# Attention's TensorE work written out in rounds of like forms, with score products that alternate between row halves

## The chip, the cores and the metric

The kernel runs on one core of a Trainium2 chip. The time is that of one execution on the device in microseconds; the median of three runs stands for the kernel. The core's engines work side by side, each through its own queue: TensorE (PE in the profile, with its weight loads as PEld), VectorE (DVE), ScalarE (ACT), GpSimd (POOL) and SyncE (SP), which here only issues DMAs. [...]

## The reference

Four blocks follow each other, each adding to x of 4 x 256 rows with 512 columns: attention, a feed-forward block with a choice of clusters, a state-space mixer over a sequence of 256, and the feed-forward block again. The change touches attention only:

```python
x = x + attn_a(layernorm(x))     # 4 batches, 256 queries, 32 heads of 16
# attn_a: q, k, v = split(x @ w_attn.T); rotary on q and k
#   y  = softmax(causal(q k^T / 4)) @ v
#   y += gating * softmax(q ak^T / sqrt(512)) @ av     # 10 adapter keys
#   return y @ w_proj.T
x = x + ffn(layernorm(x))
x = x + mixer(layernorm(x))
x = x + ffn(layernorm(x))
```

## The kernel before

Everything is float32. To keep accuracy at a higher rate, most operands are split into two fp32r parts (`split`, L104 and L105), and a product of split operands is three products (`mm3`, L112 to L114). The mixer, which takes the larger part of the time, and the last feed-forward block lie behind attention and are the same in both kernels.

Attention handles one batch b after another. A batch has eight steps u of four heads each, so there are 32 of them (`i` in the loop). For each pair of steps `pieces` (L380, L382) turns stacked parts of q and k so that four head pairs stand on partitions: 64 rows are one head with its parts, so two heads (`pr` 0 and 1) lie in the upper and lower half of the partitions.

One step consists of these parts, and each lags behind the one before it by a step:

- `scores`: for each half c of the queries and each row half pr, two products of 64 rows against all 256 keys (L425) into one PSUM tile sc, then the causal mask as one product in bf16 with the identity (L429). VectorE takes the maximum (L434), and ScalarE two exponentials with their sums (L437). For c = 0 only the first 128 keys are read.
- `turn`: twelve transposes of the exponentials (ptr, L452) in three PSUM tiles, two copied by VectorE and one by ScalarE (L453).
- `weigh`: eight value products (py, L462 and L468), each in one quarter of the array's columns, and a copy by ScalarE (ys, L473).
- `gathered`: two transposes back (try, L479), division by the sums (L485).

In every second step there are the adapter's scores (pa, L390, copied as sa, L394, turned as tra, L397). Beside this, generators give further work. `prepared(b + 1)` normalises the next batch and projects it to q, k and v (tr and pq; rotary reads pq three times on VectorE, L281 to L285). `adapter` makes the adapter's keys and values once (pk, pv). `adapted(b)` makes the softmax over the adapter's scores and its products (L496 to L520: pt, paT, pya, ya). `closed` and `ended` turn the finished y and project it (L530, po). `fed` runs the feed-forward block of finished tiles (pd).

The order in which the program is written is not the order in which engines work. A planner of the framework orders each engine's instructions, with its own costs and due times, and so mixes the parts of several steps on every engine. PSUM is divided into pools: `ps` with two buffers (tag "m") for most products, `ps_s` with three for sc, `ps_t` with two for ptr and `ps_y` with one for py. A tile takes its pool's buffers in turn and waits until the last reader of its buffer is done.

Of the kernel before, what the change touches and what calls it, by code (L numbers as in the profile page):

```python
# [20 lines left out]
P = 128  # L21
# [5 lines left out]
NA = 10  # L27
# [50 lines left out]
def hybrid_kernel(  # L78
# [153 lines left out]
    def attention(later):  # L232
        with ExitStack() as es:
# [6 lines left out]
            ps = pool("a_m", 2, space=PSUM)  # L240
            ps_s = pool("a_s", 3, space=PSUM)
            ps_t = pool("a_t", 2, space=PSUM)
# [114 lines left out]
            def prepared(b):  # L357

                where = (ps, "m") if b else (ps_s, "sc")
                xs = []  # L360
                for c in range(2):
                    xs.append(normed(norm, 2 * b + c))
                    yield
                    for f, w in ((0, wq_s), (1, wk_s)):
                        qk[b, c, f] = rotated(projected(xs[c], w, where), c, f, f"r{f}{c}")
                        yield
                for c in range(2):
                    nc.scalar.copy(vs[b % 2][:, c, :C], projected(xs[c], wv_s, where))
                    yield
# [16 lines left out]
            def adapter_scores(b, q):  # L386
# [6 lines left out]
                sa = p1.tile([AW, 4, P], F32, name="sa", tag="paT").rearrange("p s i -> p (s i)")[:, :L]  # L393
                nc.scalar.copy(sa, pa)  # L394
                tr = ps.tile([P, 2, AW], F32, name="tra", tag="m")
# [8 lines left out]
            def begin(b):  # L404
                state[b] = {
                    "as": p2.tile([P, 2, NH, NA], F32, name="as"),
# [6 lines left out]
            def scores(b, u):  # L413
# [4 lines left out]
                for c in range(2):  # L418
                    n = (c + 1) * P
                    for pr in range(2):  # L420
                        rows = slice(64 * pr, 64 * pr + 64)
                        sc = ps_s.tile([P, 2, L], F32, name="sc", tag="sc")
                        for j in range(2):
                            blk = (u % 2) * 2 + j
                            nc.tensor.matmul(  # L425
                                sc[:, j, :], qT[rows, blk, c * P : (c + 1) * P], kT[rows, blk, :],
                                start=(j == 0), stop=False,
                            )
                        nc.tensor.matmul(  # L429
                            sc[:, :, n - P : n], identb, negb.unsqueeze(1).to_broadcast([P, 2, P]),  # L430
                            start=False, stop=True,
                        )
                        nm = p3.tile([P, 2], F32, name="nmx", tag="nmx")
                        nc.vector.tensor_reduce(nm, sc[:, :, :n], AX.X, ALU.max, negate=True)  # L434
                        for j in range(2):
                            h = 4 * u + 2 * j + pr
                            nc.scalar.activation(  # L437
                                es_[c][:, 2 * j + pr, :], sc[:, j, :n], AF.Exp,
                                bias=nm[:, j : j + 1], accum_out=rs[:, c, h : h + 1],
                            )  # L440
                return es_

            def turn(es_):
# [3 lines left out]
                for src, k, dst in (  # L447
                    (es_[0], 0, e0[:, :, :P]), (es_[1], 0, e0[:, :, P:]), (es_[1], 1, e1)
                ):
                    pt = ps_t.tile([P, 4, P], F32, name="ptr", tag="pt")  # L450
# [39 lines left out]
            def adapted(b):  # L490
# [13 lines left out]
                yield  # L504
                for c in range(2):
# [6 lines left out]
                    paT = p1.tile([80, 4, P], F32, name="paT", tag="paT")  # L512
                    nc.scalar.copy(paT, pt)
                    pa = ps.tile([P, C], F32, name="pya", tag="m")
                    for s in range(4):
                        nc.tensor.matmul(
                            pa[:, s * P : (s + 1) * P], paT[:, s, :], avbd[:, s, :],
                            start=True, stop=True,
                        )
                    nc.scalar.copy(st["ya"][:, c, :], pa)  # L520
                    yield

            def closed(b, k):

                st = state[b]
                y = st["y"][:, :, k * P : (k + 1) * P]
                nc.vector.tensor_tensor(y, y, st["ya"][:, :, k * P : (k + 1) * P], ALU.add)
                tr = ps.tile([P, L], F32, name="try2", tag="m")
                for c in range(2):
                    nc.tensor.transpose(tr[:, c * P : (c + 1) * P], y[:, c, :], ident)  # L530
                split([v[:, k, :] for v in st["yT"]], tr)

            def ended(b):
# [27 lines left out]
            def fed(f, t):  # L561
                xs = normed(f.norm, t)
                yield
                f.tile(t, xs, [ps.tile([P, FH], F32, name="pd", tag="m") for _ in range(2)])
                yield
# [32 lines left out]
            def adapter():  # L598
                split(wt, wte_s)
                adapter_weights()  # L600
                adapter_scores(0, 0)
                yield
                adapter_values()
                yield
# [3 lines left out]
            for i in range(n + 3):  # L608
                if i < n:
                    b, u = divmod(i, 8)  # L610
                    if u == 0:
                        begin(b)
                        pieces(b, 0)
                        if i == 0:
                            jobs.append(adapter())
                        if b + 1 < B:
                            jobs.append(prepared(b + 1))
                    if u == 6:
                        jobs.append(adapted(b))
                    es_[i] = scores(b, u)  # L620
                    if u % 2 == 0 and i > 0:
                        adapter_scores(b, u // 2)
# [587 lines left out]
```

## Time and profile before

| | |
|---|---|
| median of three runs | 1920.82 us (1916.88 to 1924.34) |
| the profiled execution | 1916.66 us |
| its span, first to last instruction | 1914.9 us |
| granted TensorE clock over the span | 0.990 |
| first score product, start of the 32nd step, count of clusters | 36.1, 352.2 and 395.1 us |
| busy from 40 to 364 us: PE, DVE, ACT, POOL | 321.2, 203.2, 210.7, 52.3 us |

The profile's page gives each engine's busy time and its share of the span, then the span in 40 slices of 47.9 us as digits in tenths. Groups of instructions are named by line, engine, operation and tiles, result first. Each has its count, its busy time, the mean duration of one, and the idle time before it with the engine that ended it. Durations of products overlap, as TensorE works on several at once; how fast they follow each other is seen from their start times in the timeline. In a timeline's row stand start, duration from the first start to the last end of the merged instructions, engine, line, operation, tiles, shape and count. A product of two fp32 operands that is not a transpose stands there as two records.

### The profile page before, as it was taken

Reading aid. Unit: us, or ns where it says so; the run is one execution under the profiler, and the core shown is the slowest. Engines: PE = TensorE matmul, PEld = TensorE weight load, DVE = VectorE, ACT = ScalarE, POOL = GpSimd, SP = SyncE. Lnnn points to the kernel's source line nnn. Section 1 sums busy time; section 2 is a strip of 40 time slices with the busy share of each in tenths; the row PEclk is TensorE's granted clock in tenths of the full one; section 3 lists DMA queues with packets and bytes.
Section 4 is the critical chain, followed back from the end, with each engine's and each line's share of the span. In section 5 each row is a group of like instructions: output and inputs, shape, how many; then the busy total and the mean of one; then the engine's idle time right before and its main releaser. Section 6 shows DMA issues by size and latency. Waiting matters only on the chain.

```text
span 1914.9 us, 29954 instructions
## 1 busy us (share of the span) xinstructions
PE 1866.0 (97%) x10690; PEld 1468.9 (77%) x10690; DVE 1475.2 (77%) x2324; ACT 1383.2 (72%) x2873; POOL 361.0 (19%) x308
## 2 busy tenths in 40 slices
PE   7999999989999999999999999999999999999997
PEld 6767767767777787888787878877777788787786
DVE  5556657678998777877877797778777877877777
ACT  5665667557898677876787787778677877786753
POOL 4212120011331111222111121212111211131100
PEclk7999999989999999999999999999999999999999
DMA  4000000014455554544455454446454554455341
GB/s 141 1 1 1 1 21 24 12 38 155 169 192 184 160 168 140 160 154 160 149 164 161 149 172 156 148 147 187 149 165 154 160 159 160 138 166 162 119 123 49
DMA packets 151909, 240.35 MB, mean 126 GB/s; under 512 B 12368, under 2 KB 77520, under 8 KB 151760
## 3 DMA queue, kind: packets, MB, share of 16 engines
q1 hardware_dynamic: 151760, 238.44, 39.1%
q8 instruction: 84, 1.38, 0.3%
q14 instruction: 65, 0.53, 0.1%
HBM read 202.75 MB, written 35.65 MB: 124 GB/s over the span
## 4 chain that ended last, share of the span: by engine, by line
PE 84%; DVE 6%; ACT 4%; DMA 2%; issue 1%; SPq 0%; DVEq 0%; ACTq 0%
PE pp L112 12%; PE pp L113 11%; PE pp L114 11%; PE pyy L928 8%; PE pog L112 6%; PE pog L114 6%; PE pog L113 6%; PE sc L425 3%; PE trx L913 3%; PE ptr L452 2%; DVE acc L854 2%; PE py L462 1%; PE sc L429 1%; PE trp L380 1%; DMA wor<-in_wout_dram 1%
## 5 line engine op out<-in xcount | busy, mean ns | idle before, releaser
L112 PE MATMUL pp<-mx,w 128*128 128x512 f32 (+1 forms) x1160 | 465.6, 401 | 8.4 <-DVE acc L854 7.9
L114 PE MATMUL pp<-mx,w 128*128 128x512 f32 (+1 forms) x1160 | 454.2, 392 | 0.0
L113 PE MATMUL pp<-mx,w 128*128 128x512 f32 (+1 forms) x1160 | 454.2, 392 | 0.0
L854 DVE SCALAR_TENSOR_TENSOR acc<-pp,cw_s,acc 128x1012 f32<-128x1012 f32 (+2 forms) x240 | 304.8, 1270 | 23.1 <-ACT acc L847 22.4
L902 DVE TENSOR_TENSOR em<-em,gm 128x1536 f32<-128x1536 f32 x128 | 228.4, 1785 | 94.3 <-ACT em L896 86.0
L112 PEld LDWEIGHTS pp<-mx,w 128*128 128x128 f32 x1160 | 218.6, 188 | 66.0 <-issue 9.9
L114 PEld LDWEIGHTS pp<-mx,w 128*128 128x128 f32 x1160 | 218.5, 188 | 45.5 <-issue 0.4
L113 PEld LDWEIGHTS pp<-mx,w 128*128 128x128 f32 x1160 | 218.9, 189 | 40.7 <-issue 0.7
L890 POOL TENSOR_SCALAR_AFFINE_SELECT r<-r 128x512 f32<-128x512 f32 x128 | 144.6, 1129 | 526.6 <-DMA r<-cumd 418.5
L951 POOL TENSOR_TENSOR sq<-sq,acc 128x1024 f32<-128x1024 f32 x55 | 132.6, 2410 | 581.8 <-ACT acc L950 581.8
L104 ACT CAST w<-wr 128x512 fp32r<-128x512 f32 x144 | 88.5, 615 | 187.6 <-PE pp L113 164.4
L112 PE MATMUL pog<-wo,gh 128*128 128x512 f32 x512 | 204.3, 399 | 0.0
L114 PE MATMUL pog<-wo,gh 128*128 128x512 f32 x512 | 200.3, 392 | 0.0
L113 PE MATMUL pog<-wo,gh 128*128 128x512 f32 x512 | 199.9, 390 | 0.0
L895 ACT ACTIVATE em<-r,col_t 128x128 f32<-128x128 f32 x512 | 165.0, 391 | 48.2 <-PE pyy L928 46.5
L928 PE MATMUL pyy<-em,xd 128*64 128x256 f32 (+1 forms) x2048 | 189.1, 330 | 2.4 <-DVE em L902 2.4
L928 PEld LDWEIGHTS pyy<-em,xd 128*64 128x64 f32 x2048 | 134.2, 137 | 63.6 <-issue 21.7
L898 ACT ACTIVATE em<-r,col_t 128x128 f32<-128x128 f32 x512 | 166.5, 389 | 0.0
L886 DVE TENSOR_SCALAR em<-r,col_t 128x128 f32<-128x128 f32 x512 | 137.1, 327 | 12.1 <-PE pyy L928 10.1
L914 DVE TENSOR_TENSOR xd<-trx,dt_t 128x512 f32<-128x512 f32 x128 | 86.2, 683 | 54.6 <-PE trx L913 54.4
L105 DVE TENSOR_TENSOR w<-wr,w 128x512 fp32r<-128x512 f32 x139 | 97.4, 702 | 37.8 <-ACT w L104 37.3
L437 ACT ACTIVATE e<-sc,nmx 128x128 f32<-128x128 f32 (+1 forms) x256 | 105.2, 424 | 15.0 <-DVE nmx L434 14.9
(287 smaller groups left out, 3313.4 us busy)
## 6 DMA issues: line engine op xcount, KB each, us to landing
wr<-in_win_dram SPq DMA_DIRECT2D x287, 256.0 KB, 2.8
r<-cumd SPq DMA_DIRECT2D x128, 512.0 KB, 4.1
spill<-gb SPq DMA_DIRECT2D x63, 512.0 KB, 2.8
gr<-spill SPq DMA_DIRECT2D x120, 256.0 KB, 3.5
wor<-in_wout_dram SPq DMA_DIRECT2D x64, 256.0 KB, 3.1
out_dram<-x SPq DMA_DIRECT2D x8, 256.0 KB, 2.3
x<-in_x_dram SPq DMA_DIRECT2D x1, 1536.0 KB, 10.2
gr<-spill SPq DMA_DIRECT2D x8, 192.0 KB, 2.5
```

The costliest lines, as they stand in the source:

```text
L112: nc.tensor.matmul(o, lh, rh, start=(first and k == 0), stop=False)
L113: nc.tensor.matmul(o, lh, rl, start=False, stop=False)
L114: nc.tensor.matmul(o, ll, rh, start=False, stop=(last and k == n - 1))
L437: nc.scalar.activation(es_[c][:, 2 * j + pr, :], sc[:, j, :n], AF.Exp, bias=nm[:, j : j + 1], accum_out=rs[:, c, h : h + 1],)
L854: nc.vector.scalar_tensor_tensor(av[:, :, d:], pv[:, :, : L - d], cw_s[:, ch, tap : tap + 1], av[:, :, d:], ALU.mult, ALU.add,)
L886: nc.vector.tensor_scalar(e[:, b, 2, :], rv[:, b, 1, :], col_t[:, h, b, 1:2], 0.0, ALU.subtract, ALU.min,)
L890: nc.gpsimd.affine_select(rv[:, :, 0, :], rv[:, :, 0, :], pattern=[[0, B], [1, P]], compare_op=ALU.is_ge, fill=-1e30, base=0, channel_mult ...
L895: nc.scalar.activation(e[:, b, 1, :], rv[:, b, 1, :], AF.Exp, bias=col_t[:, h, b, 2:3])
L898: nc.scalar.activation(e[:, b, 0, :], rv[:, b, 0, :], AF.Exp, bias=col_t[:, h, b, 0:1])
L902: nc.vector.tensor_tensor(e, e, gm, ALU.mult)
L928: nc.tensor.matmul(py[d, b, k * P :], xd[:, 2 * b + k, d], es2[hh][:, b, 2 * k : 2 if k == 0 else 3, :].rearrange("p s i -> p (s i)"), sta ...
L951: (nc.gpsimd if n < NB - 1 else nc.vector).tensor_tensor(sq, sq, x2, ALU.add)
```

## The change

The diff does four things.

1. Inside `tc.manual_schedule` TensorE's instructions keep the order in which the program writes them. The other engines are still ordered by the planner. The loop is written as rounds: scores; one long job (`step("long", i)`: a projection, the output projection, a feed tile, adapter keys or values); the adapter's scores; the transposes of the round before; back transposes; further transposes (`step("turn", i)`); the adapter's value products; the value products of two rounds before in one run; the next pieces. A generator moves at most one stage in a round.
2. In `scores` the eight products come in a run, c = 1 first, alternating between the two row halves, which write to two PSUM tiles. Then come the four masks. For c = 0 the products take only the first 128 keys, and the tile is half as wide.
3. PSUM: `ps` gets three buffers and takes the ptr tiles too, `ps_s` gets four, `ps_t` goes.
4. Smaller ones: sa and paT have two buffers, the adapter's scores (as) one, nmx six; both copies of paT come ahead of the products pya; `closed` takes the turns of three parts together and includes `ended`; the feed-forward block is set up two rounds later (`n - 6`), and its tiles are begun one in a round from round 28 on. The pieces of the next batch's first pair are made in round 6 of the batch before.

```diff
-            ps = pool("a_m", 2, space=PSUM)
-            ps_s = pool("a_s", 3, space=PSUM)
-            ps_t = pool("a_t", 2, space=PSUM)
+            ps = pool("a_m", 3, space=PSUM)
+            ps_s = pool("a_s", 4, space=PSUM)
...
-                sa = p1.tile([AW, 4, P], F32, name="sa", tag="paT").rearrange("p s i -> p (s i)")[:, :L]
+                sa = p2.tile([AW, 4, P], F32, name="sa", tag="paT").rearrange("p s i -> p (s i)")[:, :L]
                 nc.scalar.copy(sa, pa)
+                yield
                 tr = ps.tile([P, 2, AW], F32, name="tra", tag="m")
...
-                for c in range(2):
+                made = []
+                for c in (1, 0):
                     n = (c + 1) * P
-                    for pr in range(2):
-                        rows = slice(64 * pr, 64 * pr + 64)
-                        sc = ps_s.tile([P, 2, L], F32, name="sc", tag="sc")
-                        for j in range(2):
-                            blk = (u % 2) * 2 + j
+
+                    pair = [ps_s.tile([P, 2, n], F32, name="sc", tag="sc") for _ in range(2)]
+                    for j in range(2):
+                        blk = (u % 2) * 2 + j
+                        for pr in range(2):
+                            rows = slice(64 * pr, 64 * pr + 64)
                             nc.tensor.matmul(
-                                sc[:, j, :], qT[rows, blk, c * P : (c + 1) * P], kT[rows, blk, :],
-                                start=(j == 0), stop=False,
+                                pair[pr][:, j, :], qT[rows, blk, c * P : (c + 1) * P],
+                                kT[rows, blk, :n], start=(j == 0), stop=False,
                             )
-                        nc.tensor.matmul(
-                            sc[:, :, n - P : n], identb, negb.unsqueeze(1).to_broadcast([P, 2, P]),
-                            start=False, stop=True,
+                    made += [(c, pr, sc) for pr, sc in enumerate(pair)]
+                for c, pr, sc in made:
+                    n = (c + 1) * P
+                    nc.tensor.matmul(
+                        sc[:, :, n - P :], identb, negb.unsqueeze(1).to_broadcast([P, 2, P]),
+                        start=False, stop=True,
+                    )
+                    nm = p3.tile([P, 2], F32, name="nmx", tag="nmx", bufs=6)
+                    nc.vector.tensor_reduce(nm, sc, AX.X, ALU.max, negate=True)
+                    for j in range(2):
+                        h = 4 * u + 2 * j + pr
+                        nc.scalar.activation(
+                            es_[c][:, 2 * j + pr, :], sc[:, j, :], AF.Exp,
+                            bias=nm[:, j : j + 1], accum_out=rs[:, c, h : h + 1],
                         )
...
-                    pt = ps_t.tile([P, 4, P], F32, name="ptr", tag="pt")
+                    pt = ps.tile([P, 4, P], F32, name="ptr", tag="m")
...
+            with tc.manual_schedule(engines={nc.tensor.engine}):
+                for i in range(n + 7):
                     b, u = divmod(i, 8)
-                    if u == 0:
-                        begin(b)
-                        pieces(b, 0)
+                    if i < n:
                         if i == 0:
-                            jobs.append(adapter())
-                        if b + 1 < B:
-                            jobs.append(prepared(b + 1))
...
+                        es_[i] = scores(b, u)
+                    if i == n - 6:
+                        inner.close()
...
+                    if slow and i >= n - 4:
+                        begun(slow.pop(0))
+                    step("long", i)
+                    if i < n and u % 2 == 0 and i > 0:
+                        asides.append(adapter_scores(b, u // 2))
+                        next(asides[-1])
+                    if 1 <= i <= n:
+                        eTs[i - 1] = turn(es_.pop(i - 1))
+                    if 3 <= i < n + 3:
+                        gathered(*divmod(i - 3, 8), yss.pop(i - 3))
+                    while asides:
+                        next(asides.pop(0), 0)
+                    step("turn", i)
+                    if i < n and u == 7:
+                        begun(adapted(b))
+                    step("values", i)
+                    if 2 <= i <= n + 1:
+                        yss[i - 2] = weigh(*divmod(i - 2, 8), eTs.pop(i - 2))
...
+                    if i < n and u % 2 == 0:
+                        if u < 6:
+                            pieces(b, u // 2 + 1)
+                        elif b + 1 < B:
+                            pieces(b + 1, 0)
```

## The prediction

> **What bounds the kernel now.** I read the page first: busy shares, then the slices, then the costliest groups.
>
> ```profile
> PE 1866.0 (97%) x10690; PEld 1468.9 (77%) x10690; DVE 1475.2 (77%) x2324; ACT 1383.2 (72%) x2873; POOL 361.0 (19%) x308
> PE   7999999989999999999999999999999999999997
> PEclk7999999989999999999999999999999999999999
> ```
>
> TensorE is busy 97% of the span and in slices 1 to 7 (48 to 383 us), where attention lies, nearly all the time. The change touches attention alone: its first score product starts at 36.1 us (of the 1914.9) and its last step, the count of clusters, at 395.1. So 359 us are at stake; the mixer behind them keeps its work. The next question is who makes TensorE wait there. The list of waits between 48 and 364 us, for TensorE alone, is all of this:
>
> ```profile
> PE pya L516 <- ACT paT L513: 0.7, 1, 0.7
> PE sc L425 <- ACT e L437: 0.3, 1, 0.3
> PE ptr L452 <- ACT e L437: 0.2, 1, 0.2
> PE ptr L452 <- DVE eT L453: 0.2, 1, 0.2
> ```
>
> It waits 1.4 us in 316. Attention is bound by what TensorE is given and by the order it gets it in. Busy is not the same as streaming, though, and this is read from start times in the timeline (start, duration, what):
>
> ```profile
> 80.97 0.62 PE L462 MATMUL py<-eT,av 128*32 128x256 f32 x2
> 81.52 0.36 PE L397 MATMUL tra<-con,sa 80*128 80x80 f32 x2
> 81.81 0.42 PE L462 MATMUL py<-eT,av 128*32 128x256 f32 x3
> ...
> 82.59 0.44 PE L479 MATMUL try<-con,ys 128*128 128x128 f32 x2
> ...
> 91.46 0.64 PE L462 MATMUL py<-eT,av 128*32 128x256 f32 x8
> 91.91 0.40 PE L468 MATMUL py<-eT,av 128*32 128x128 f32 x8
> 92.25 0.44 PE L479 MATMUL try<-con,ys 128*128 128x128 f32 x2
> ...
> 95.41 0.50 PE L425 MATMUL sc<-pc,pc 64*128 64x256 f32 x2
> 95.84 0.28 PE L429 MATMUL sc<-negb,identb 128*128 128x256 bf16 x1
> 96.06 0.50 PE L425 MATMUL sc<-pc,pc 64*128 64x256 f32 x2
> 96.49 0.28 PE L429 MATMUL sc<-negb,identb 128*128 128x256 bf16 x1
> 96.70 0.50 PE L425 MATMUL sc<-pc,pc 64*128 64x256 f32 x2
> ```
>
> One score group (two products of 64 rows, one mask) repeats every 0.64 us (96.06 to 96.70). The products hold 0.43 of it: in the trace the second starts 0.22 behind the first and the mask 0.21 behind the second. A 256-column product in full-array form repeats in 0.12 (the adapter's pa, L390). So about 0.10 per product is not streaming: the weights of a product in the same half are loaded after the product before it, and each change between the 64-row and the full form costs about 0.10. The value products py show the same: in one piece they hold 0.79 us (91.46 to 92.25); cut in two by the planner they hold 0.55 + 0.78 = 1.33 (80.97 to 81.52, 81.81 to 82.59).
>
> **The change, part by part.** A round is one u of one batch; there are 32.
>
> *Scores.* Today four groups, 4 x 0.645 = 2.58 us. After: eight products in a run, alternating between the halves, then four masks in a run. No row of this trace has two row halves side by side. The nearest is py, whose four column quarters start 5 to 7 ns apart in the trace, so they run at once. If halves behave so, each half repeats in 0.22 and two products are done in it. Products with all keys: 2 x 0.22 = 0.44. Those of the first queries now stream 128 columns; load 0.11 + stream 0.06 = 0.17 per pair, 0.34. With 0.10 to enter the form: 0.88. Masks 4 x 0.11 = 0.44. Together 1.32, saving 1.26 a round, 40 us in all. If halves merely hide each other's loads, one product every 0.11, it is the same 0.88. If they share nothing, 8 x 0.22 = 1.76: the saving is 12.
>
> *128 columns.* An fp32r product this narrow is not in the trace. [...]
>
> *Value products.* Always in one piece: 0.79 and 0.09 to enter, against 1.33 or more; 0.5 x 32 = 16 us. TensorE's own saving: 40 + 16 = 56.
>
> *What fixed order and buffers give back.* Now the planner fills TensorE's gaps. After, it stands in its queue. PSUM goes from 2 + 3 + 2 + 1 banks to 3 + 4 + 1: transposed weights (ptr), projections, pieces (trp), adapter and transposes share three buffers in turn. I walk a round from its first score product, in us; a round's eight exponentials follow each other by 0.45 (256 columns) or 0.34 (128), 3.16 in all, beginning 1.85 after it (products, mask, 0.6 of maximum), so they end at 5.0.
>
> - Rounds with a projection: scores to 1.3, twelve products at 0.233 to 4.1. VectorE reads pq three times, 1.3 us, to 5.65. The third of the next uses of the buffers is a ptr group at about 5.0: it waits 0.7. Some 18 rounds: 13 us. The projection is the cover: it carries TensorE past the exponentials, behind which ScalarE's copies sa and eT stand.
> - Even rounds without one (8, 16, 24, 26): pa is done at 1.8, but its copy sa stands on ScalarE behind the exponentials until 5.35. The third ptr group needs that buffer and waits from 2.7 to 5.4; behind it stand try, the adapter's transposes, py and the next pieces. About 3 us each with what follows: 12.
> - Adapter softmax, once per batch: maximum 0.81, POOL 1.29, exponential 0.74 stand in ScalarE's order ahead of the copies of the pieces; about 1 each, 4.
> - Round 0: pk comes right behind the first masks (now at 47.5), but the adapter weights take 6.6 us from its end to the last copy (51.0 to 57.6) with TensorE's queue behind them. Some of it is won back as pk comes 8 us sooner (clock, below): net 3.
>
> Other moves: the buffer swaps (as to one, paT to two, six nmx) cost nothing while nobody reads the old copy that late. Feed tiles start in round 28 instead of 24, so 144 of their 192 products follow the last round's scores, in place of 72: from that round's first score to the count it is 42.9 us today (352.2 to 395.1), and after, by the rows above, 38 of work and today's 6 of idle, so nothing. DMA issues stay the same ones on SP's queue; those of the feed weights come two rounds later, still three rounds ahead of their use (they land in 3.6 us).
>
> Sum: 56 - (13 + 12 + 4 + 3) = 24 us. The profiled execution took 1916.7 (span and 1.8 around it) and goes to 1892.7; the median of the runs is 4.2 above, 1920.8 to 1896.8. I say 1896.
>
> [...] The clock first, from the windows view (us, busy PE, PEld, DVE, ACT, POOL with counts, clock, DMA):
>
> ```profile
> 32.00:36.00 4.00, 1.77 (x12) 1.40 (x12) 2.60 (x3) 1.95 (x6) 2.95 (x5) 0.87 0.00 2
> 36.00:48.00 12.00, 11.50 (x45) 7.97 (x45) 5.39 (x11) 8.03 (x30) 0.92 (x3) 0.50 0.00 1
> 114.00:137.00 23.00, 22.91 (x181) 16.17 (x179) 14.36 (x30) 18.41 (x64) 2.30 (x5) 1.00 0.00 1
> ```
>
> [...] Rounds 24 to 27 will have transposes, scores and py but no projection for about 30 us. From 36 to 48 such a mix did stay at 0.50 after the idle of 32 to 36. From 114 to 137 the same mix without one wide projection kept 1.00. [...]
>
> **Rivals.**
> (A) The waits are hidden: copies come in time, three buffers suffice. Speaking for it: DVE and ACT are busy only 203 and 211 of the 324 us from 40 to 364. Against: the copies' order behind the exponentials. 56 less 5: 1870.
> [...]
> (C) The halves share nothing: 12 + 16 - 32, 1925. For it: within one half a product takes 0.22; against: the quarters of py run at once.
> (D) Slower. One mechanism: TensorE in its fixed order waits for ScalarE's copies behind the exponentials, in every round, not only the light ones. It decides above 56 / 32 = 1.75 us a round; at 2.5 it is 80 us and 1945. For it: today's order has 1.4 us of waits because the planner moves other work in; against: a projection of 2.8 us stands between scores and copies in most rounds.
>
> **How the numbers follow.** My forecast 45% (own range 1880 to 1908), A 20%, B 15%, C 12%, D 8%. Measured no change is within 0.5%, 1911.2 to 1930.4, since the runs of the kernel before spread by 0.4%. Faster: 45 + 20 + 13 of B = 78. Same: 2 of B, 8 of C = 10. Slower: the rest, 12. The range for 8 in 10 runs from 1862, below A, to 1926, C's middle and the narrow products at their high price.
>
> **What would show it.** Right: scores of a round with masks in about 1.3 us, products of the two halves starting within some 10 ns or 0.11 apart; py near 0.8; TensorE's list of waits in attention at 25 to 40 us, led by sa, eT and the projection's reads on VectorE; the count near 371. Wrong: the 128-column products more than 0.2 apart; clock 0.50 after round 8; waits over 60 us, or under 10.

## The result and the profile after

The changed kernel takes 1903.41 us, the kernel before, timed beside it, 1919.88: a ratio of 0.9915, 95% interval 0.9901 to 0.9929. It is 16.5 us faster. The forecast was 1896 and its range 1862 to 1926. The profiled execution spans 1900.1 us, 14.8 less than before.

The page of the changed kernel: busy time, the slices of 47.5 us each, and the shares of the chain of work that ended last.

```profile
PE 1817.5 (96%) x10690; PEld 1452.2 (76%) x10690; DVE 1477.0 (78%) x2324; ACT 1381.4 (73%) x2873; POOL 350.2 (18%) x308
PE   7988889889999999999999999999999999999997
PEclk8999999989999999999999999999999999999999
PE 77%; DVE 9%; ACT 8%; DMA 2%; issue 2%; POOL 1%; SPq 0%; DVEq 0%; ACTq 0%; POOLq 0%
```

The last of these lines for the kernel before:

```profile
PE 84%; DVE 6%; ACT 4%; DMA 2%; issue 1%; SPq 0%; DVEq 0%; ACTq 0%
```

TensorE is busy 48.5 us less than before (1866.0), and the kernel is only about a third of that faster. In the slices of attention, where there were nines, there are now eights: TensorE waits. The chain ran over TensorE for 84% of the span before; now it is 77%, and the copying engines have taken the rest (DVE 6 to 9, ACT 4 to 8).

What TensorE's time in attention consists of is worked out from start times: a product is charged with the time from its start to the start of the next one, less idle over 70 ns, which is charged to waits. "Wide" are products of 512 or 288 columns (projections, feed). The stretch runs from the first score product to the count of clusters; behind it both kernels take 1520 to 1521 us. The last column is the time, from start to start, of the products that started at a granted clock of 0.50. All in us; each ratio is to the kernel before as timed beside that kernel. The experiments stand here too and are told below.

| kernel | median, ratio to before | stretch | score | mask | py | wide | other | waits | at 0.50 |
|---|---|---|---|---|---|---|---|---|---|
| before | 1919.9 | 359.1 | 58.8 | 19.5 | 41.5 | 110.1 | 120.8 | 8.3 | 12.7 |
| after | 1903.4, 0.9915 | 343.5 | 20.8 | 13.3 | 27.3 | 108.7 | 132.2 | 41.3 | 26.5 |
| e1, halves in turn | 1904.0, 0.9914 | 345.0 | 21.6 | 13.2 | 27.1 | 110.4 | 131.1 | 41.6 | 29.2 |
| e6, all keys | 1904.5, 0.9917 | 343.5 | 22.5 | 12.6 | 27.1 | 109.0 | 131.3 | 41.0 | 23.1 |
| e8, new scores in the kernel before | 1907.5, 0.9938 | 350.3 | 48.4 | 17.9 | 37.0 | 113.1 | 124.8 | 9.1 | 24.1 |
| e2, planner's order | 1896.9, 0.9876 | 337.8 | 39.4 | 14.4 | 39.5 | 108.8 | 122.9 | 13.0 | 10.2 |
| e10, planner, runs kept whole | 1901.6, 0.9907 | 337.8 | 20.8 | 13.1 | 25.9 | 106.2 | 130.7 | 41.1 | 15.8 |
| e12, fourth shared buffer | 1884.2, 0.9818 | 326.1 | 20.3 | 13.2 | 26.2 | 111.0 | 123.8 | 31.5 | 26.7 |
| e7, rounds 24 to 27 filled | 1901.6, 0.9909 | 343.6 | 20.4 | 12.6 | 26.1 | 109.2 | 137.7 | 37.6 | 20.0 |
| e4, feed early | 1899.8, 0.9894 | 340.8 | 20.3 | 12.7 | 26.9 | 108.5 | 131.8 | 40.5 | 23.2 |
| e14, e12 and e4 | 1876.1, 0.9777 | 317.0 | 20.4 | 13.5 | 25.4 | 108.3 | 123.2 | 26.3 | 19.9 |
| e13, e12, e4 and e2 | 1873.6, 0.9763 | 313.8 | 36.5 | 15.0 | 25.4 | 105.9 | 118.4 | 12.7 | 8.3 |

So scores, masks and value products gave 58.4 us, waits took 33.0 of it back and the other work 10.0 (other +11.4, wide -1.4). The difference, 15.4, is the gain.

Most of those 10.0 belong to the waits as well. The last product ahead of a wait is charged with its whole duration (a ptr with 273 ns, where without a wait the next one starts 118 ns after it). There are 84 such products after and 17 before, and what they are charged above the mean of their kind is 11.9 us after and 2.5 before. So waits delayed TensorE by 42.4 us more than before, and 33.0 is the idle part of it.

The list of waits of the changed kernel between 36 and 379 us, TensorE alone, its first seven rows: what waited, for whom, us in total, times, longest.

```profile
PE try L484 <- DVE eT L458: 6.0, 9, 1.0
PE ptr L457 <- DVE t L284: 4.0, 6, 0.7
PE ptr L457 <- DVE eT L458: 3.9, 6, 1.0
PE tra L332 <- POOL st L305: 2.5, 2, 1.7
PE try L484 <- ACT av L368: 2.4, 3, 0.8
PE ptr L457 <- ACT av L368: 2.1, 3, 0.7
PE ptr L457 <- ACT sa L393: 2.1, 5, 0.7
```

All but the fourth are a tile in the shared pool with tag "m" of PSUM, where TensorE's products land; the releaser in each of their rows is a step that reads an older tile of that pool (eT reads ptr, t and av read pq, sa reads pa; in round 8, below, VectorE's first copy ends at 113.41 and the waiting ptr group starts at 113.47). None of them is longer than 1.7 us; they are many small ones, in nearly every round.

One round, number 8, is a light one without a projection. The timeline of the changed kernel: TensorE from its first score product to the next round's (start, duration, what, count, idle before and its releaser).

```profile
109.94 0.67 PE L427 MATMUL sc<-pc,pc 64*128 64x256 f32 x8
110.54 0.61 PE L434 MATMUL sc<-negb,identb 128*128 128x256 bf16 x4
110.91 0.73 PE L389 MATMUL pa<-pc,akbd 128*80 128x256 f32 x4
111.47 1.04 PE L457 MATMUL ptr<-con,e 128*128 128x128 f32 x8
113.47 0.66 PE L457 MATMUL ptr<-con,e 128*128 128x128 f32 x4 [0.96 <-DVE eT L458]
114.15 0.41 PE L484 MATMUL try<-con,ys 128*128 128x128 f32 x2
115.21 0.36 PE L397 MATMUL tra<-con,sa 80*128 80x80 f32 x2 [0.65 <-DVE ry L489]
115.40 1.04 PE L515 MATMUL pt<-con,as 128*80 128x128 f32 x8
116.68 0.66 PE L163 MATMUL tr<-con,axn 128*128 128x128 f32 x4 [0.23 <-ACT paT L519]
117.26 0.64 PE L467 MATMUL py<-eT,av 128*32 128x256 f32 x8
117.72 0.40 PE L473 MATMUL py<-eT,av 128*32 128x128 f32 x8
118.05 1.85 PE L379 MATMUL trp<-con,st 128*128 128x128 f32 x16
119.83 0.38 PE L427 MATMUL sc<-pc,pc 64*128 64x256 f32 x2
```

And the same stretch on ScalarE:

```profile
114.44 0.40 ACT L442 ACTIVATE e<-sc,nmx 128x128 f32<-128x128 f32 x1
114.69 0.24 ACT L442 ACTIVATION_READ_ACCUMULATOR e<-sc,nmx 128x1 f32 x1
114.78 0.38 ACT L393 COPY sa<-pa 80x256 f32<-80x256 f32 x1
115.03 0.61 ACT L458 COPY eT<-ptr 128x512 f32<-128x512 f32 x1
```

Eight score products come in one run; first product to first mask is 0.60 us, the masks to pa another 0.37. Two ptr groups begin together, the third waits 0.96 for VectorE's copy of the first, which stands behind the four maxima:

```profile
110.86 1.95 DVE L439 TENSOR_REDUCE nmx<-sc 128x2 f32<-128x512 f32 x4 [1.08 <-PE sc L434]
112.73 1.28 DVE L458 COPY eT<-ptr 128x512 f32<-128x512 f32 x2
```

The adapter's transposes tra wait 0.65. The trace puts that down to ry on VectorE, but sa, which they read, is copied at 114.78, behind the last exponential, and ends at 115.16: that is what released them at 115.21, 0.05 later.

### The profile page after: what moved, and what is told of

The parts are those of the page before. It is cut to its first block, busy times and chain, and to the rows that moved or that the text cites. A ratio compares the mean times of both kernels' runs of the same rounds, so it can differ in the third digit from the quotient of the medians.

```text
span 1900.1 us, 29893 instructions
## 1 busy us (share of the span) xinstructions
PE 1817.5 (96%) x10690; PEld 1452.2 (76%) x10690; DVE 1477.0 (78%) x2324; ACT 1381.4 (73%) x2873; POOL 350.2 (18%) x308
## 4 chain that ended last, share of the span: by engine, by line
PE 77%; DVE 9%; ACT 8%; DMA 2%; issue 2%; POOL 1%; SPq 0%; DVEq 0%; ACTq 0%; POOLq 0%
PE pp L112 12%; PE pp L113 12%; PE pp L114 11%; PE pyy L961 8%; PE pog L112 6%; PE pog L114 6%; PE pog L113 6%; PE trx L946 3%; ACT e L442 3%; DVE acc L887 2%; DMA wor<-in_wout_dram 1%; PE ptr L457 1%; PE sc L427 1%; DVE nmx L439 1%; PE py L467 1%
## 5 line engine op out<-in xcount | busy, mean ns | idle before, releaser
L887 DVE SCALAR_TENSOR_TENSOR acc<-pp,cw_s,acc 128x1012 f32<-128x1012 f32 (+2 forms) x240 | 304.9, 1270 | 23.2 <-ACT acc L880 22.6
L112 PEld LDWEIGHTS pp<-mx,w 128*128 128x128 f32 x1160 | 218.5, 188 | 65.6 <-issue 10.2
L923 POOL TENSOR_SCALAR_AFFINE_SELECT r<-r 128x512 f32<-128x512 f32 x128 | 133.7, 1045 | 542.8 <-DMA r<-cumd 441.2
L442 ACT ACTIVATE e<-sc,nmx 128x256 f32<-128x256 f32 (+1 forms) x256 | 103.7, 431 | 24.9 <-DVE nmx L439 24.9
```

What stands on the lines that cost most here:

```text
L112: nc.tensor.matmul(o, lh, rh, start=(first and k == 0), stop=False)
L442: nc.scalar.activation(es_[c][:, 2 * j + pr, :], sc[:, j, :], AF.Exp, bias=nm[:, j : j + 1], accum_out=rs[:, c, h : h + 1],)
L887: nc.vector.scalar_tensor_tensor(av[:, :, d:], pv[:, :, : L - d], cw_s[:, ch, tap : tap + 1], av[:, :, d:], ALU.mult, ALU.add,)
L923: nc.gpsimd.affine_select(rv[:, :, 0, :], rv[:, :, 0, :], pattern=[[0, B], [1, P]], compare_op=ALU.is_ge, fill=-1e30, base=0, channel_mult ...
```

## Experiments

All are edits of the changed kernel, but for e8, which edits the kernel before.

### Is it the alternation of the halves? (e1)

```diff
-                for c in (1, 0):
-                    ...
-                    for j in range(2):
-                        for pr in range(2):
+                for pr in range(2):
+                    rows = slice(64 * pr, 64 * pr + 64)
+                    for c in (1, 0):
+                        for j in range(2):
```

The four products of the upper half come first, then the four of the lower.

> Same eight score products, masks behind them and fixed order, but all four of the upper row half first, then the four of the lower one. In the changed kernel the pairs of the two halves start 3 to 4 ns apart, 0.22 us behind the pair before (256 columns) and 0.11 (128). Theory (the halves run at once and that is where the score saving lies): each half then takes 0.22 + 0.22 + 0.11 alone and the second follows the first, some 0.65 more in a round, 32 x 0.65 = 21 us, less what lies in waits anyhow: 15 to 21 slower than the changed kernel, 1918 to 1925. Rival (the gain comes from grouping products and masks, fewer changes between the 64-row and the full form): 5 us or less, up to 1908.

Measured: 1904.04 us against 1903.41, ratios 0.9914 and 0.9915. So the alternation is not what pays. The timeline of e1 shows a run of nearly the same length (0.63 from its start to the first mask, where the changed kernel has 0.60):

```profile
164.84 0.70 PE L428 MATMUL sc<-pc,pc 64*128 64x256 f32 x8
165.47 0.61 PE L435 MATMUL sc<-negb,identb 128*128 128x256 bf16 x4
```

The starts inside one such run, in ns from its first product (worked out from the trace):

```
after  (halves alternate)   0   3 | 222 226 | 342 345 | 402 405 | mask 608
e1     (upper, then lower)  0  13 | 222 236 | 341 353 | 401 414 | mask 617
before (one half, two products)  0   224 | mask 432
```

In the kernel before two products of one half start 0.22 apart. In e1 products start in pairs 13 ns apart although the second half's first product stands four places behind the first half's first. The widths say the same: in the program the upper half's two narrow products stand ahead of the lower half's two wide ones, but in all 32 runs of e1 the four wide ones start first and the four narrow ones behind them. So in these runs the starts of one half did not wait for the products of the other that stand ahead in the program. (A trace names neither the half nor the place in the queue; the reading rests on TensorE being given the order of the program, as item 1 of the change has it.) The first step of a half is 0.22 in all three; what the longer run adds is that the later ones are 0.12 and 0.06. What the changed kernel and e1 have in common is that eight products of both halves stand in one run without a mask between them; score takes 20.8 and 21.6 us there, against 58.8 before.

### What are the narrow products worth? (e6)

```diff
-                    pair = [ps_s.tile([P, 2, n], F32, name="sc", tag="sc") for _ in range(2)]
+                    pair = [ps_s.tile([P, 2, L], F32, name="sc", tag="sc") for _ in range(2)]
...
-                                kT[rows, blk, :n], start=(j == 0), stop=False,
+                                kT[rows, blk, :], start=(j == 0), stop=False,
```

The first queries get products with all 256 keys again; only the first 128 columns are read.

> The changed kernel with the first queries' products over all 256 keys again, in tiles of full width; fixed order and runs stay. [...]

Measured: 1904.48, ratio 0.9917 (0.9901 to 0.9933): 1.1 us above the changed kernel, where the author had estimated some 7 for the wider products, less what waits take in. A run takes 674 ns to its first mask against 608, so the narrow products save 0.066 us a round, 2 us in all (score 22.5 against 20.8), and the median does not show it. In the changed kernel a narrow pair is followed after 60 ns, a wide one after 120. Only this one step of a run gets shorter, and the high price of narrow products that the range allowed for did not come.

### The new scores alone, in the kernel before (e8)

```diff
-                    for pr in range(2):
-                        rows = slice(64 * pr, 64 * pr + 64)
-                        sc = ps_s.tile([P, 2, L], F32, name="sc", tag="sc")
-                        for j in range(2):
+                    pair = [ps_s.tile([P, 2, n], F32, name="sc", tag="sc") for _ in range(2)]
+                    for j in range(2):
+                        for pr in range(2):
...
+                    for pr, sc in enumerate(pair):
+                        nc.tensor.matmul(                      # mask
```

Planner, pools and loop stay as they were.

> The kernel before with the new scores alone: pairs of row halves in a run with 128 keys for the first queries, masks behind each pair of tiles; old loop, old pools (2, 3, 2, 1), TensorE ordered by the planner. Theory (both halves beside each other are the gain; fixed order and pools give nothing net): the score part falls from 78 to 45 to 55 us, waits stay near 10: 1893 to 1902. Rival (the gain needs the fixed order or the new pools): the planner parts the halves again, 1910 to 1920.

Measured: 1907.5, ratio 0.9938 (0.9920 to 0.9956), between the two expectations. The planner cuts most of the runs: score falls to 48.4, not to 20.8. Waits stay at 9.1. So about 12 of the 16.5 us can be had with one function and without any of the order.

### What does the fixed order do? (e2, e10)

e2 gives TensorE's order back to the planner and leaves all else as in the changed kernel:

```diff
-            with tc.manual_schedule(engines={nc.tensor.engine}):
+            with ExitStack():
```

> The changed kernel without the fixed order: same program, same pools, TensorE ordered by the planner again. Theory (the fixed order costs some 33 us of waits, but keeps py and the score runs whole): TensorE's waits in attention fall from 41 towards 8 to 15 us, its work rises as score runs and py are cut again (the compiled order shows both cut in many rounds); what it returns is 10 to 25 of the 30 won: 1895 to 1915, near the changed kernel. Rival 1 (fixed order is the loss): 1880 or less. Rival 2 (fixed order is the gain, whatever the scores do): back to 1915 to 1925.

Measured: 1896.94, ratio 0.9876 (0.9861 to 0.9890), 7 us faster than with the order written out. The timeline of e2 shows what the planner does with a score run (cut by transposes at 160.60) and with a value run (cut at 166.36):

```profile
159.76 0.60 PE L379 MATMUL trp<-con,st 128*128 128x128 f32 x5
160.29 0.38 PE L427 MATMUL sc<-pc,pc 64*128 64x256 f32 x2
160.60 0.53 PE L379 MATMUL trp<-con,st 128*128 128x128 f32 x4
161.06 0.43 PE L427 MATMUL sc<-pc,pc 64*128 64x128 f32 x3
161.43 0.61 PE L434 MATMUL sc<-negb,identb 128*128 128x256 bf16 x4
...
165.59 0.64 PE L467 MATMUL py<-eT,av 128*32 128x256 f32 x8
166.05 0.38 PE L473 MATMUL py<-eT,av 128*32 128x128 f32 x2
166.36 0.66 PE L457 MATMUL ptr<-con,e 128*128 128x128 f32 x4
166.95 0.42 PE L473 MATMUL py<-eT,av 128*32 128x128 f32 x6
```

It cuts scores and value products (104 and 70 pieces where the fixed order has 32 and 32), and each cut costs: score +18.6, py +12.2, mask +1.1. But the pieces in between are work that was ready: waits fall by 28.3 and other work by 9.3 (what is charged there to products ahead of waits fell by 9.9). The second outweighs the first by 5.7 us in the stretch. The low clock has a share in this too: 10.2 us at 0.50 in place of 26.5.

Is it the cutting itself that hides the waits? e10 keeps the planner and pins only the score products and the value products in the order of the program:

```diff
-                            nc.tensor.matmul(
+                            tc.keep_in_program_order(nc.tensor.matmul(
```

> The changed kernel with TensorE ordered by the planner, but score products and py pinned to the order of the program, so that each of the 32 rounds has one run of eight score products and one of eight py (the planner alone made 104 and 70). Theory (what the fixed order wins is whole runs, what it costs is waits of everything else): score part near 34 and py near 27 us as in the changed kernel, waits near 13 to 20 as with the planner: 1872 to 1886. Rival (cut runs are what hides the waits): waits return in place of the cuts, 1894 to 1903.

Measured: 1901.59, ratio 0.9907 (0.9891 to 0.9924). All 32 score runs and 32 value runs are whole, and the waits are back, 41.1 us. But this does not answer the question. In the trace of e10 TensorE's products of the stretch follow each other in the order of the changed kernel, one by one (2405 records against 2408, three of pk are missing). The planner was left no room by the pins, or used none: for TensorE e10 is the changed kernel once more. Whether the runs can be whole and the waits hidden with three shared buffers stays open; with four, e13 below has its value runs whole and 12.7 us of waits.

For the clock e10 tells more. The profiled execution took 1896.3, five below the median, with the same order and the same waits as the changed kernel. The windows view of the stretch in both, the changed kernel first (us, then busy PE, PEld, DVE, ACT and POOL with counts, granted clock, DMA share, GB/s):

```profile
35.80:379.30 343.50, 301.86 (x2408) 237.42 (x2409) 223.84 (x505) 225.22 (x795) 54.62 (x86) 0.96 0.03 9
35.50:373.40 337.90, 296.33 (x2407) 234.86 (x2407) 223.59 (x505) 223.98 (x795) 54.77 (x86) 0.98 0.03 9
```

Products at 0.50 take 15.8 us in place of 26.5, and the stretch is 5.7 us shorter. So 10.7 us at the low clock cost about half of themselves, and how much of it an execution gets is not settled by the order alone.

### Are the waits a matter of PSUM buffers? (e12)

```diff
-            ps = pool("a_m", 3, space=PSUM)
+            ps = pool("a_m", 4, space=PSUM)
...
-            ps_y = pool("a_y", 1, space=PSUM)
...
-                py = ps_y.tile([P, L], F32, name="py", tag="py")
+                py = ps.tile([P, L], F32, name="py", tag="m")
```

The same eight buffers (3 + 4 + 1 before, 4 + 4 now), but the one that was py's alone is now shared by all.

> The changed kernel with four shared PSUM buffers instead of three: py gives up its own and takes one of them. Theory (most of the 41 us of waits in attention are for a buffer, whose last reader is a copy on VectorE or ScalarE behind maxima and exponentials: those put down to eT, rotary reads, av and sa, about 20 us): waits fall by 8 to 15, 1889 to 1897. Rival (TensorE waits for results, not for buffers, and py now stands in the same queue for buffers): waits within 4 of 41, 1899 to 1907.

Measured: 1884.17, ratio 0.9818 (0.9799 to 0.9838): 19 us faster than the changed kernel, and better than expected. The order of TensorE's products is the same, one by one, so this is not a matter of order. Waits fall from 41.3 to 31.5 and other work from 132.2 to 123.8. The transposes ptr follow each other in 120 ns instead of 133 at full clock, as 16 of them stand ahead of a wait in place of 36, and in round 8 all twelve stand in one run. The list of waits of e12 in attention, its first three rows, and round 8:

```profile
PE tra L396 <- ACT sa L392: 4.5, 4, 1.3
PE py L466 <- ACT av L367: 4.2, 3, 1.4
PE try L483 <- DVE eT L457: 3.1, 4, 1.7
```

```profile
107.79 1.48 PE L456 MATMUL ptr<-con,e 128*128 128x128 f32 x12
109.80 0.44 PE L483 MATMUL try<-con,ys 128*128 128x128 f32 x2 [0.53 <-DVE eT L457]
111.54 0.36 PE L396 MATMUL tra<-con,sa 80*128 80x80 f32 x2 [1.30 <-ACT sa L392]
```

The third ptr group waits no more. What is left in such a round is the wait for sa, the copy behind the exponentials: tra waits for a result there and not for a buffer. The shortage of buffers was a cause of the waits, and not the only one.

### Does the clock fall for want of work? (e7)

In rounds 24 to 27, 16 more products of 256 columns each, into a py buffer; nobody reads them.

```diff
+                    if i in (24, 25, 26, 27):
+                        wm = ps_y.tile([P, L], F32, name="wm", tag="py")
+                        for _ in range(16):
+                            nc.tensor.matmul(wm, wp_s[0][:, 0, :P], wp_s[0][:, 0, :L], start=True, stop=True)
```

> Sixteen further products of 256 columns, whose result nobody reads, ahead of the transposes in each of the rounds 24 to 27: 4 x 16 x 0.11 = 7 us of work more. Theory (these rounds lose time to the halved clock, 10 us at 0.50 between 272 and 289, and to waits of about 1.5 each): the clock stays at 1.00 there, which wins 5, and the waits take in about 4 of the 7, so nothing in sum: 1900 to 1905. Rival (the clock falls anyway, or costs nothing): 3 to 7 slower, 1906 to 1910.

Measured: 1901.58, ratio 0.9909 (0.9892 to 0.9925), no slower than without this work. The windows view from 266 to 300 us (us, then busy PE, PEld, DVE, ACT and POOL with counts, granted clock, DMA share, GB/s), first of the changed kernel:

```profile
266.00:280.00 14.00, 11.32 (x101) 8.66 (x97) 9.84 (x20) 12.14 (x40) 1.79 (x4) 0.88 0.17 45
280.00:300.00 20.00, 17.73 (x152) 13.36 (x154) 12.77 (x29) 15.56 (x61) 1.79 (x4) 0.83 0.01 2
```

and of e7:

```profile
266.00:280.00 14.00, 13.21 (x129) 11.69 (x130) 10.52 (x21) 12.95 (x44) 1.76 (x4) 1.00 0.17 46
280.00:300.00 20.00, 18.86 (x194) 15.72 (x193) 12.48 (x30) 15.41 (x58) 1.79 (x4) 1.00 0.00 1
```

With more to do the clock stays at 1.00 there. In e1, e6 and e10, which give TensorE the same kinds of work in these rounds as the changed kernel, it was 0.50 for 3.4 to 6.8 us between 266 and 300, and in the changed kernel for 10.2. 64 products of about 0.12 are 7.7 us of work, and the stretch is as long as before (343.6 and 343.5): partly the work lies in former waits (37.6 against 41.3), partly the full clock pays for it (20.0 us of the stretch at 0.50, against 26.5).

### When does the feed-forward block begin? (e4)

```diff
-                    if i == n - 6:
+                    if i == n - 8:
...
-                    if slow and i >= n - 4:
+                    if slow and i >= n - 7:
```

> Feed-forward block set up in round 24, its tiles begun from round 25 on, one in a round, three rounds sooner than in the changed kernel. Batch 3 (start of its first scores to the count) takes 113.3 us in the changed kernel and 110.6 before. Theory (light rounds 24 to 27 pay with waits and with the clock, 10 us of them at 0.50): rounds 26 and 27 get a feed tile as cover, the clock stays at 1.00 there, worth 5 to 8 us; but the tail loses its cover, worth 2 to 4 back: 1896 to 1902. Rival (work is only moved from tail to light rounds): 1902 to 1906.

Measured: 1899.84, ratio 0.9894 (0.9879 to 0.9908), 3.6 us faster than the changed kernel, within what was expected. From the first score product of the last round to the count it is now 35.2 us, where the changed kernel has 48.6, with 72 feed products instead of 144. Most of that is work moved forward, not saved; in the stretch as a whole 2.7 us are gone.

The same edit on top of e10:

> As the run with pinned score products and py, and the feed-forward tiles begun three rounds sooner. Theory: the planner fills light rounds by itself, so it is worth 0 to 3 us less than there; rival (light rounds hold the end of attention in both): 4 to 8 less.

Measured: 1898.77, ratio 0.9885 (0.9865 to 0.9906), 2.8 us below e10. TensorE's products come in the order of e4 (but for three records of pk), so this is e4 once more and says nothing of the planner. And on top of e2:

> Planner's order on TensorE (1896.9 so far) and feed-forward tiles begun three rounds sooner (won 3.6 in the fixed order). Theory (light rounds 24 to 27 cost in both): 1892 to 1895. Rival (the planner had already spread the tiles): 1895 to 1899.

Measured: 1894.73, ratio 0.9873 (0.9856 to 0.9890), against e2's 0.9876: no difference that can be told. An early feed seems to help where TensorE has waits that it can fill, but by so little that each step lies near the width of its interval.

### Put together (e14, e13)

e14 joins the fourth shared buffer and the early feed under the fixed order; e13 does the same with the planner's order.

> The changed kernel in its fixed order with four shared buffers and the feed-forward tiles three rounds sooner. Theory: the gains of both add, 3.6 and 6 to 14: 1886 to 1894. Rival (they cover the same waits): no better than the better of the two alone.

> The same with four shared buffers, py among them. Theory of buffers: the planner's remaining 13 us of waits are mostly the tail and the start, so a fourth buffer gives 0 to 4: 1889 to 1895; rival (py in the shared buffers makes the planner part more runs): 1897 to 1905.

Measured: e14 1876.11, ratio 0.9777 (0.9760 to 0.9793); e13 1873.63, ratio 0.9763 (0.9749 to 0.9778). Both are some 10 and 15 us faster than expected. The edits add up, and more: e12 had given 19 us against the changed kernel and e4 3.6, together 23, and e14 is 27 faster. e13 is the fastest kernel here, 45 us ahead of the kernel before and 30 ahead of the changed one. Its scores stand in 94 pieces, but its 32 value runs are whole, and its waits are 12.7 us: whole value runs and hidden waits go together here.

With four buffers the planner's order is worth only some 2.5 us more than the fixed one, with intervals that overlap, where it had been worth 7 with three (5 with the early feed, e9 against e4). A likely reason is that fewer waits are left for it to fill (26.3 us in e14, 40.5 in e4).

## Why the prediction was right or wrong

The forecast of the sum, 24 us, was 15.4 in the profiled stretch, and this is how its terms came out. "At full clock" is the mean of a product's kind at a clock of 1.00 with no wait behind it; the price of the low clock is what products at 0.50 took above it. All in us.

| | before | after | change | forecast |
|---|---|---|---|---|
| scores, masks, value products at full clock | 117.3 | 56.8 | -60.5 | -56 |
| wide and other work at full clock | 226.2 | 221.6 | -4.6 | 0 |
| waits: idle | 8.3 | 41.3 | +33.0 | +32, all of a wait |
| waits: charged to the product ahead | 2.5 | 11.9 | +9.4 | |
| low clock | 4.7 | 12.0 | +7.3 | 0 |

The mechanism was right: TensorE's time falls, and waits for copies take half and more of it back. That the number came so near is in part luck. Waits cost 10.4 us more than forecast and the clock 7.3, and 9.1 us that were not counted on (4.5 in scores and value products, 4.6 in the rest) paid for half of that.

**Scores and masks: right, slightly more.** Forecast from 2.58 to 1.32 us a round, 40 us. Measured 44.2. At full clock a score product takes 76 ns of TensorE in place of 222, a mask 95 in place of 149: 8 x 0.076 + 4 x 0.095 = 0.99 a round. The forecast had 0.22 for each wide pair and 0.17 for each narrow one, with a load in every step; only the first pair takes 0.22, the next follow by 0.12 and 0.06. The 0.06 that the forecast puts down for the stream of 128 columns was the author's estimate, and so was the high price in its range: no run of the kernel before shows a product of this form. In the changed kernel a narrow pair is followed 60 ns later. The halves start 3 ns apart, near the 5 to 7 of the quarters of py from which this was forecast. Rival C (halves that share nothing) and the high price are refuted by the run's starts and e6. That the two halves must *alternate* was not said, and e1 shows that they need not.

**Value products: right.** Forecast -16, measured -14.2: 49 ns a product at full clock (0.79 for the 16), against 81.

**What the waits give back: too little, and in other places.** Forecast 32. Idle time alone rose by 33.0 (8.3 to 41.3), but the walk counts how much later the next product starts, and by that measure it was 42.4: there are many waits, and each has its share in the product ahead. By rounds the idle time was:

| | forecast | measured, idle |
|---|---|---|
| light even rounds 8, 16, 24, 26 | 12 | 1.8 + 1.7 + 1.6 + 0.9 = 6.0 |
| round 0 | 3 (net) | 3.4, of it 2.5 for POOL's st |
| all 26 other rounds but the last | 13 in 18 projection rounds, 4 for the adapter's softmax | 24.4, 0.9 a round |
| last round | no more than today's 6 | 7.4 |

The step of 0.7 us in projection rounds is there in the size that was walked out (ptr behind VectorE's t, L284: 4.0 us, 6 times, longest 0.7), but in 6 rounds, and 3 more behind ScalarE's av, not 18. In the odd rounds with little long work, 3, 11, 19, 25 and 27, there is a wait that the walk did not have: the back transposes try wait 1.0 each time for a buffer that VectorE's copy eT still reads, five of the 9 cases and 5.0 of the 6.0 us in the list.

The light rounds failed at a named step: "the third ptr group needs that buffer", pa's. In round 8 the third group begins at 113.47, before pa is copied at 114.78. It took the buffer of the first ptr group, and what it waited for was VectorE, which copies that group behind the four maxima, not ScalarE. The sentence that a tile takes its pool's buffers in turn, on which the walk leaned and which the description of the kernel before has too, is not what this trace shows. The order behind the exponentials that the step named is real: e12 has it bare, 1.3 us of tra behind sa.

**Work counted at nothing: the clock.** Products at a granted clock of 0.50 took 26.5 us of the stretch instead of 12.7 (from 36.3, 46.6, 145.6, 193.4, 271.9 and 282.1 us on). That cost 7.3 us more than before, and e10, with the same order and 10.7 us less of it, was 5.7 shorter. The forecast has no term for this, in line with a row of the kernel before (23 us with no wide product at 1.00). That row was of a TensorE that is busy 22.91 of 23 us; the same kind of work with waits in it, 11.32 busy of 14, had 0.88. The want of wide products alone does not describe it either: the changed kernel has 14.2 us without a wide product from 212.8 to 227.0 at full clock. What stood ahead of the four falls after round 8 was 3.4 us with much idle time (columns as in the windows of e7):

```profile
142.20:145.60 3.40, 1.45 (x9) 0.76 (x8) 2.31 (x5) 3.40 (x16) 0.00 (x0) 1.00 0.00 0
190.00:193.40 3.40, 1.75 (x13) 1.07 (x11) 2.69 (x7) 3.40 (x18) 0.00 (x0) 0.99 0.00 0
268.50:271.90 3.40, 1.75 (x13) 1.22 (x13) 2.70 (x7) 3.40 (x17) 0.00 (x0) 1.00 0.06 5
278.70:282.10 3.40, 2.24 (x18) 1.76 (x17) 2.80 (x7) 3.40 (x17) 0.61 (x2) 1.00 0.02 5
```

From 220.6 to 224.0 TensorE was busy for 2.24 us as well and the clock stayed, so no threshold follows from this. In e7, with 16 more products in each of the rounds 24 to 27, the clock was 1.00 from 266 to 300. They fill idle time and change the mix of work, and no run parts the two; the four rows speak for the idle time, and the question stays open.

**Other work.** Of its +11.4, 9.0 are the products ahead of waits and 3.5 the low clock; at full clock it fell by 1.1.

**Last round.** "So nothing" was 4.6 too low: 48.6 us from its first score product to the count, not 38 + 6. Waits were 7.4 there, work 41.2. The count of feed products behind that point today was also wrong, 96, not 72. e4, which moves feed products ahead of that point, was 3.6 faster.

**Rivals.** A (waits hidden) is refuted by the list of waits; B, which had 1906 to 1911 for dearer narrow products or a halved clock in rounds 24 to 27, came nearest in time and named the right place, as one of several (10.2 us at 0.50 there), while its narrow products at 60 ns did not come dear; D's waits exist in every round as it said, at 42.4 / 32 = 1.3 us a round, below its 1.75. Of the marks set beforehand, masks and scores, the halves' distance, and py hold; the list of waits, which counts those over 150 ns, holds too with 39.7 (25 to 40), led by eT and by the projection's reads t as it said, but not by sa; the count is at 379.3, not 371; and the clock's 0.50 after round 8, which was to count as wrong, did come.

## What to carry to other kernels

Count what an order hides as well as what it costs: the planner's cut-up runs (e2) cost 32 us of score, mask and value time, but they stood in the place of 28 us of waits and of 9 more, most of which were the same waits charged to the products ahead of them. Measure a wait by how much later the next product starts; idle time alone showed 33 of 42 us here. When such waits appear, look for the buffers that they are queued for before ordering anything by hand: here one PSUM buffer, moved from a private pool into the shared one on top of the change, was worth more than the change itself (19 against 16.5 us); in the kernel before it was not tried. And a row that says "the clock holds in this mix" speaks for an engine as busy as in that row (22.91 of 23 us, at 1.00); with waits in the mix the clock did not hold here (11.32 of 14, at 0.88).

## What the runs showed of the hardware

- The starts in the two row halves did not follow the order between the halves: with all four products of the upper half first in the program, the lower half's first product still started 13 ns after the upper's, and the four wide products of both halves started ahead of the four narrow ones (e1, all 32 runs).
- In a run with both halves (changed kernel and e1) the second product of a half started 0.22 us behind its first, as in the kernel before, but the later ones 0.12 behind one of 256 columns and 0.06 behind one of 128. Whether a run of one half alone would show this too, no run here tells.
- In this mix, in the changed kernel, the clock fell to 0.50 for 3.4 or 6.8 us at a time, amid waits of 0.2 to 1.7 us, and came back at 196.8, 275.3 and 288.9 us before any wide product had come. The same order of products had 26.5 us of it in one execution and 15.8 in another (changed kernel, e10), and was 5.7 us shorter with the less.
